# A decoder layer on one core: PSUM handed out bank by bank, gate and up products apart, waits for transfers written as pieces of their own

## The chip, the cores and the metric

The kernel runs on one core of a Trainium2 chip. The metric is the device time of one execution in microseconds; three executions of the kernel before took 1224.41 to 1229.97 us, with a median of 1229.68 us. Five engines work side by side, each through its own instructions in order: TensorE (PE, matrix products, results to PSUM), VectorE (DVE), ScalarE (ACT), GpSimd (POOL) and SyncE (SP, which here issues nearly all transfers). They wait for one another through semaphores.

## The reference

One pre-norm decoder layer on x of 4 sequences x 1024 positions x 256 channels, in float32: causal self-attention with 16 heads of 16 channels, cross-attention to a context of 77 positions with a mask, and a gated feed-forward layer of 768 hidden channels with integer weights. Cut to what is computed:

```python
Q, K, V = x @ Wq.T + bq, x @ Wk.T + bk, x @ Wv.T + bv      # per head h
scores = (gt * (Q @ W_cross) @ K.T + (1 - gt) * Q @ (M @ K).T) * scale
attn = softmax(where(causal, scores, -inf)); out = (attn @ V) @ Wo.T + bo
...
q, k, v = query @ Wq, ctx @ Wk, ctx @ Wv                   # cross-attention
attn = softmax(where(masked, -1e9, q @ k.T / sqrt(16))); out = (attn @ v) @ Wo
...
h = silu(x @ wg.T) * (x @ wu.T); out = h @ wd.T            # feed-forward
...
x = x + self_attn(layernorm(x))
x = x + cross_attn(layernorm(x), ctx, mask)
x = x + ffn(layernorm(x))
```

## The kernel before

The 4 sequences are each cut into two chunks of 512 rows, so there are eight chunks (b, n). For each chunk six things happen. `project` normalises the rows, transposes them and makes q, k and v; q and k are split into a high and a low part (`spread`), which are copied by transfers into the row layout that the score products read. `maxima` multiplies q by k and takes each row's maximum on VectorE (L879), which `shift` turns into a tile of shifts. `attend` computes the scores again the other way round, adds the shifts by another product (L955), takes the exponential on ScalarE (L968) and multiplies by v (`weigh`, L992); `quotients` divides, and `out_proj` multiplies by the output weights and adds the residual (L722). `cross_attention` does the same against the context, with score maxima at L1114 and L1120. `ffn` computes gate and up products for six blocks of 128 hidden channels (L1229), tanh on ScalarE (L1235), two multiplications on VectorE (L1236, L1237), a split into high and low parts on ScalarE and GpSimd (L1239, L1240), and then the down products (L1263), which VectorE adds to x (L1269).

The order of TensorE's instructions is not that of these functions. Each function is a generator that yields pieces. A piece states how long TensorE needs for it (`pe`), which engines work on its result and for how long (`use`), which buffers it takes, and from what time on (`at`) or under what condition (`cond`) it may start. `weave` keeps a planned time for every engine and buffer and always writes next the piece that could start first, after a small correction per stream and chunk (`LATES`). What is written is then fixed: on the chip each engine runs its instructions in that order and waits by semaphores. Work of other engines that belongs to a piece is written with it, so it also stands in the order in which pieces are chosen.

PSUM has eight banks of 512 float32 values per partition. Before, three pairs of banks (`pair`) and two single banks (`single`) are rotating buffers, and the planner keeps the same numbers of slots:

```python
pp = ctx.enter_context(tc.tile_pool(name="pp", bufs=3, space=PSUM))
ps = ctx.enter_context(tc.tile_pool(name="ps", bufs=2, space=PSUM))
...
"pair": Slots(3), "single": Slots(2), "es": Slots(6), ...
```

A gate product and its up product share one pair; so do the four row blocks of `out_proj`, of the v projection and of the down products, each of which is read by one VectorE instruction of 1024 columns (v: four ScalarE copies).

Three further places matter. In `late_weights` the selection tiles `sel` and `selB` (L524 to L536) are made after the first head group of `maxima` has been started (flag "begun"), and the mask of the first sequence (L1047 to L1049) inside `load_cross`. `load_ffn` loads, converts and transposes the feed-forward weights from the flag "selections" on. In `attend` the residual rows x are loaded and the bias `bo_b` is added to them on GpSimd (L922) at the chunk's first head group. A layer norm is statistics on VectorE (L153, L154, L156), a power on GpSimd (L158) and four normalisations on VectorE (L166), written in one go.

Of the kernel before, what the change touches and what calls it, by code (L numbers as in the profile page):

```python
# [8 lines left out]
F32 = mybir.dt.float32  # L9
# [4 lines left out]
AF = mybir.ActivationFunctionType  # L14
# [13 lines left out]
def tile_decoder_layer(  # L28
# [53 lines left out]
    pp = ctx.enter_context(tc.tile_pool(name="pp", bufs=3, space=PSUM))  # L82
    ps = ctx.enter_context(tc.tile_pool(name="ps", bufs=2, space=PSUM))

    def pair():
        return pp.tile([P, 2, CH], F32, tag="pair", name="pair")

    def single():
        return ps.tile([P, CH], F32, tag="single", name="single")
# [81 lines left out]

    def layer_norm(xt, keep=None):

        mv, rs = row_scales(xt, keep)
        return normal_rows(xt, mv, rs, wide([P, QT, D], "xn"))
# [215 lines left out]
    class Slots:  # L391
# [12 lines left out]

    slots = {
        "pair": Slots(3), "single": Slots(2), "es": Slots(6), "w4": Slots(6), "f2": Slots(6),
# [50 lines left out]
    def give(token, when):  # L457
        pool, k = token
        pool.free[k] = when
# [7 lines left out]
    def weave(*streams, until=None):  # L467
        while True:
# [23 lines left out]
            s.got = {k: [slots[k].take() for _ in range(c)] for k, c in p["take"].items()}  # L492
            s.end = t + p["pe"]
            if p["pe"]:
                if t - tensor["end"] > REST:
                    tensor["slow"] = t + COLD
                s.end += min(max(tensor["slow"] - t, 0.0) / 2, p["pe"])
                tensor.update(end=s.end, mode=p["mode"])
# [39 lines left out]
    def late_weights(st):  # L538

        yield piece(0.0, w4=1, use=[("DVE", 4.0)], cond=lambda: "begun" in flags)  # L540
        selections(wide([P, NHP, P], "sel_f"))
        st.release("w4")
        flags.add("selections")
        nc.gpsimd.memset(mneg, 0.0)
        nc.gpsimd.memset(xpad, 0.0)
        nc.gpsimd.tensor_copy(k2s, zero.to_broadcast(k2s.shape))
        nc.gpsimd.memset(v2, 1.0)
        nc.sync.dma_start(xwo, xWo.rearrange("(n p) f -> p n f", p=P))
        yield piece(0.0, w4=3, use=[("DMA", 4.0), ("POOL", 8.0)])
        toks = st.got["w4"]  # L550
        reorder(xwq, raw_weights(xWq))
        give(toks.pop(), st.done)
        raw = raw_weights(xWk)
# [3 lines left out]
        yield piece(0.0, es=2, use=[("DMA", 4.0)])  # L557
# [43 lines left out]
        yield piece(0.0, w4=2, use=[("DMA", 4.0)])  # L601
# [22 lines left out]
    def load_ffn(st, m, rest=None):  # L624
# [5 lines left out]
        for part, n0 in enumerate(range(0, n_all, step)):  # L630
            n = min(step, n_all - n0)
            yield piece(
                0.0, w4=1, use=[("DMA", 4.0), ("POOL", 1.1), ("DVE", 1.1)],
                cond=lambda: "selections" in flags,
# [5 lines left out]
            wf = wi.bitcast(F32)  # L640
            nc.gpsimd.tensor_copy(wf, wi)
# [54 lines left out]
    NORM = [("DVE", 2.6), ("POOL", 1.1), ("DVE", 1.7)]  # L696

    def out_proj(st, nat, t_nat, w, xt):
# [7 lines left out]
        for i in range(QT):  # L706
            if i % 2 == 0:
                yield piece(
                    2.0, at=st.done + LATE if i == 0 else 0.0,
                    use=[("DVE", 1.25)] if i else [], free=t_aT if i else [],  # L710
                    **({} if i else {"pair": 1}),
                )
                if i == 0:
                    t_pair = st.got["pair"]
                    t = pair().rearrange("p a (i d) -> p (a i) d", d=D)
            for c in range(NC):
                nc.tensor.matmul(
                    t[:, i, :], aT[:, c, i * P : (i + 1) * P], w[:, c, :],
                    start=(c == 0), stop=(c == NC - 1),
                )  # L720
        give(t_pair.pop(), st.done)
        nc.vector.tensor_tensor(xt, t, xt, ALU.add)  # L722
# [57 lines left out]
    def project(st, b, n):  # L780
# [4 lines left out]
        else:  # L785
            yield piece(
                0.0, use=[("DMA", 4.0)] * (b > 0) + NORM, w4=1,
# [3 lines left out]
            xn = x01 if (b, n) == (0, 1) else x_rows(b, n)  # L791
            normal_rows(xn, *row_scales(xn))
# [8 lines left out]
        for c in range(NC):  # L801
# [8 lines left out]
            if c == 0:  # L810
                for i in range(QT):
                    if i % 2 == 0:
                        yield piece(
                            2.0, use=[("ACT", 1.8)] if i else [],
                            cond=lambda: (b, n) != (0, 0) or ("normal", 0, 1) in flags,
                            **({} if i else {"pair": 1, "v": 1}),
                        )
                        if i == 0:
                            t_pair, t_v = st.got["pair"], st.got["v"][0]
                            vs = qk.tile(  # L820
                                [P, QT, H * V1 + W - V1], F32, tag="v", name="vs", bufs=NQ
                            )
                            nc.gpsimd.memset(vs, 1.0)
                            t = pair().rearrange("p a (i d) -> p (a i) d", d=D)
                    for k in range(NC):
                        nc.tensor.matmul(
                            t[:, i, :], xnT[:, k, i * P : (i + 1) * P], wvT[:, k, :],
                            start=(k == 0), stop=(k == NC - 1),
                        )
                give(t_pair.pop(), st.done)  # L830
                for i in range(QT):
                    nc.scalar.copy(
                        vs[:, i, : H * V1].rearrange("p (h w) -> p h w", w=V1)[:, :, 0:HD],
                        t[:, i, :].rearrange("p (h w) -> p h w", w=HD),
                    )
# [531 lines left out]
```

## Time and profile before

| what | value |
|---|---|
| median of three executions | 1229.68 us |
| the profiled execution | 1232.86 us |
| its span, first to last instruction | 1231.1 us |
| mean granted TensorE clock | 0.958 |
| transfers | 76.44 MB in 65438 packets |

A group row of the profile holds line, engine, operation, tiles, shapes and count, then busy time and mean duration in ns, then the idle time of the engine just before them and what ended most of it. Rows of the timeline hold start, duration and what ran; a bracket holds the idle time before it and the instruction that ended it. Ends of matmuls are modelled, so that starts tell more of their pace than durations do.

### The profile page before, as it was taken

To read this page: it belongs to the slowest core of one execution; us is meant where nothing else is said; L and a number is where in the kernel's file an instruction comes from. 1 tells how busy PE (TensorE), PEld (TensorE's weight loads), DVE (VectorE), ACT (ScalarE), POOL (GpSimd) and SP (SyncE) were. 2 spreads that over 40 slices of the span, in tenths; PEclk is the share of its full clock that TensorE was granted. 3 is DMA by queue.
4 is the path that set the end of the run, shared out by engine and by line. 5 is a ranking of instruction groups with operands and counts; after the bars stand their busy time and mean duration, and the time that the engine had idled before them with its cause. 6 is when DMAs were issued, how large, how long until landed. Compare 5 with 4: busy or idle time off the path is not lost. (4 is left out here: it accounts for less than half of the span.)

```text
span 1231.1 us, 22029 instructions
## 1 busy us (share of the span) xinstructions
PE 1110.8 (90%) x9059; PEld 684.9 (56%) x9059; DVE 729.9 (59%) x1247; ACT 562.6 (46%) x801; POOL 130.8 (11%) x138
## 2 busy tenths in 40 slices
PE   6679989999999898999898998999999889996875
PEld 4445544557555466557555456556575545565654
DVE  5566786354687856255777856347458666136342
ACT  3044544654434463753353563653535336661521
POOL 4031000002000012001100002000110000011212
PEclk9798999999999999999999998999999989998986
DMA  6992315537732016555533015444826140006000
GB/s 124 130 201 63 58 33 69 69 53 92 97 55 40 9 38 110 75 71 87 87 52 38 8 42 70 85 63 60 102 44 91 36 63 8 18 1 86 1 35 19
DMA packets 65438, 76.44 MB, mean 62 GB/s; under 512 B 22451, under 2 KB 39399, under 8 KB 65332
## 3 DMA queue, kind: packets, MB, share of 16 engines
q1 hardware_dynamic: 64227, 74.62, 39.1%
q8 instruction: 73, 1.20, 0.5%
q10 hardware_dynamic: 1104, 0.35, 0.1%
q14 instruction: 34, 0.27, 0.1%
HBM read 15.28 MB, written 9.33 MB: 20 GB/s over the span
## 5 line engine op out<-in xcount | busy, mean ns | idle before, releaser
L968 ACT ACTIVATE es<-pair 128x1024 f32<-128x1024 f32 (+3 forms) x384 | 300.8, 812 | 252.6 <-PE pair L962 178.4
L879 DVE TENSOR_REDUCE mt<-pair 128x2 f32<-128x1024 f32 (+3 forms) x384 | 351.4, 952 | 92.3 <-PE pair L874 60.8
L866 PE MATMUL pair<-k,q 64*128 64x512 f32 (+3 forms) x768 | 163.2, 428 | 29.8 <-DVE mt L879 12.6
L949 PE MATMUL pair<-q,k 64*128 64x512 f32 (+3 forms) x768 | 161.4, 417 | 22.4 <-DVE mt L879 16.5
L992 PE MATMUL single<-es,vs 128*32 128x512 f32 (+3 forms) x1536 | 166.2, 506 | 0.1
L866 PEld LDWEIGHTS pair<-k,q 64*128 64x128 f32 x768 | 76.0, 188 | 121.4 <-DVE mt L879 41.7
L955 PE MATMUL pair<-ms,sel 64*128 64x512 f32 (+3 forms) x768 | 134.6, 347 | 0.0
L949 PEld LDWEIGHTS pair<-q,k 64*128 64x128 f32 x768 | 73.2, 187 | 102.6 <-issue 34.8
L1240 POOL TENSOR_TENSOR hT<-h,hT 128x512 fp32r<-128x512 f32 x48 | 61.4, 1280 | 306.8 <-ACT hT L1239 297.2
L1162 ACT ACTIVATE es<-pair 77x1024 f32<-77x1024 f32 x64 | 63.4, 1020 | 45.8 <-PE pair L1160 45.5
L955 PEld LDWEIGHTS pair<-ms,sel 64*128 64x128 f32 x768 | 74.2, 190 | 3.1
L1120 DVE TENSOR_REDUCE mx<-pair 128x8 f32<-128x616 f32 x64 | 48.7, 794 | 43.7 <-PE pair L1114 43.7
L1263 PE MATMUL pair<-wdT,hT 128*128 128x256 f32 x384 | 63.3, 320 | 11.6 <-POOL hT L1240 4.8
L158 POOL TENSOR_TENSOR rs<-ve,mhalf 128x4 f32<-128x4 f32 x24 | 24.3, 1012 | 439.5 <-DVE ve L156 439.4
L1235 ACT ACTIVATE h<-pair 128x512 f32<-128x512 f32 x48 | 28.7, 598 | 89.0 <-PE pair L1229 84.8
L874 PE MATMUL pair<-cm_qk,id 64*128 64x64 bf16 (+1 forms) x1024 | 69.0, 211 | 0.0
L962 PE MATMUL pair<-cm_kq,id 64*128 64x64 bf16 (+1 forms) x1024 | 67.3, 211 | 0.0
L1236 DVE SCALAR_TENSOR_TENSOR h<-h,pair 128x512 f32<-128x512 f32 x48 | 33.0, 687 | 57.5 <-ACT h L1235 57.2
L1263 PEld LDWEIGHTS pair<-wdT,hT 128*128 128x128 f32 x384 | 55.8, 216 | 18.4 <-POOL hT L1240 6.3
L1114 PE MATMUL pair<-k2s,q 128*128 128x156 f32 x256 | 46.7, 308 | 12.1 <-DMA q<-hi 5.3
L992 PEld LDWEIGHTS single<-es,vs 128*32 128x32 f32 x1536 | 32.4, 109 | 40.7 <-issue 29.6
L674 ACT COPY aS<-single 128x512 f32<-128x512 f32 x64 | 37.5, 589 | 31.6 <-PE single L992 19.0
(180 smaller groups left out, 1575.0 us busy)
## 6 DMA issues: line engine op xcount, KB each, us to landing
q<-hi SPq DMA_DIRECT2D x128, 128.0 KB, 5.1
q<-lo SPq DMA_DIRECT2D x128, 128.0 KB, 6.3
k<-hi SPq DMA_DIRECT2D x64, 128.0 KB, 4.3
k<-lo SPq DMA_DIRECT2D x64, 128.0 KB, 6.0
xr<-in_x_dram SPq DMA_DIRECT2D x8, 512.0 KB, 6.0
x<-in_x_dram SPq DMA_DIRECT2D x8, 512.0 KB, 7.4
x_dram<-x SPq DMA_DIRECT2D x8, 512.0 KB, 2.6
out_dram<-x SPq DMA_DIRECT2D x8, 512.0 KB, 3.7
```

The lines of the kernel that those rows point to most:

```text
L866: nc.tensor.matmul(t[:, j, :w], q[r, a, i * P : (i + 1) * P], k[r, a, :w], start=True, stop=True,)
L874: nc.tensor.matmul(t[:, j, w - P + 64 * half : w], id2[r, half], cm_qk[r, half, 64 * half :], start=False, stop=True, skip_group_check=True,)
L879: nc.vector.tensor_reduce(mt[:, i, :, p, kc], t[:, :, :w], AX.X, ALU.max)
L949: nc.tensor.matmul(t[:, j, lo:], k[r, a, ki * P : (ki + 1) * P], q[r, a, lo:], start=True, stop=False,)
L955: nc.tensor.matmul(t[:, j, lo:], sel[r, hp, :], ms[r, lo:], start=False, stop=True)
L962: nc.tensor.matmul(t[:, j, lo : lo + 64 * (half + 1)], id2[r, half], cm_kq[r, half, : 64 * (half + 1)], start=False, stop=True, skip_group ...
L968: nc.scalar.activation(es[:, :, lo:], t[:, :, lo:], AF.Exp)
L992: nc.tensor.matmul(acc[0][W * jj : W * (jj + 1), lo:], vs[:, ki, V1 * h : V1 * h + W], both[jj // 2][:, jj % 2, lo:], start=(kb == 0), sto ...
L1120: nc.vector.tensor_reduce(mt[:, i, h4 : h4 + 4, :].rearrange("q (k p) j -> q k (p j)", k=2), tv[:, :, :, :S2], AX.X, ALU.max,)
L1162: nc.scalar.activation(es[:S2], t[:S2], AF.Exp)
L1240: nc.gpsimd.tensor_tensor(hs[:, 1, :], h, hs[:, 0, :].bitcast(F32), ALU.subtract)
L1263: nc.tensor.matmul(t[:, i, :], h[1][:, v, i * P : (i + 1) * P], w[:, h[0], :], start=(m == 0), stop=(m == len(terms) - 1),)
```

## The change

PSUM becomes one tile of eight banks. The planner's `Banks` keeps one list of eight times when banks come free; a single takes the highest bank that is free by the plan, a pair two neighbours, even positions first. The gate product and the up product take a single each; `out_proj`, the v projection and the down products are made in two halves of one bank each, with one VectorE or ScalarE instruction per half. When the planner sees TensorE stand still for over 1.3 us and a bank is free, `stirred` writes filler products into the bank about to be used; the next product overwrites them. Statistics and normalisation, loads and the work on what they bring, become separate pieces. The selections and the first mask are made ahead of the first maxima, the feed-forward weights are loaded after the first attention, and x and its bias come at the last head group. The planned transfer time goes from 4.0 to 6.5 us in these pieces, and `LATES` has other values.

```diff
-    pp = ctx.enter_context(tc.tile_pool(name="pp", bufs=3, space=PSUM))
-    ps = ctx.enter_context(tc.tile_pool(name="ps", bufs=2, space=PSUM))
+    pp = ctx.enter_context(tc.tile_pool(name="pp", bufs=1, space=PSUM))
+    banks = pp.tile([P, 8, CH], F32, name="banks")
...
+    def stirred(t, part):
+        for _ in range(int(stand["us"] / 0.235)):
+            nc.tensor.matmul(part, selB, sel[:, 0:4, :], start=True, stop=True)
+        stand["us"] = 0.0
+        return t
+
+    def bank(kind, of):
+        if given[kind]:
+            return given[kind].pop(0)
...
     def pair():
-        return pp.tile([P, 2, CH], F32, tag="pair", name="pair")
+        b = bank("pair", 4)
+        return stirred(banks[:, b : b + 2, :], banks[:, b, :])
...
+    class Banks:
...
+        def take(self):
+            now = max(tensor["end"], self.when(1))
+            ready = [b for b in self.all() if self.at(b) <= now]
+            b = max(ready) if self.width == 1 else min(ready, key=lambda b: (b % 2, b))
+            self.give(b, 1.0e9)
+            return self, b
...
-        "pair": Slots(3), "single": Slots(2), "es": Slots(6), "w4": Slots(6), "f2": Slots(6),
+        "pair": Banks(free_banks, 2), "single": Banks(free_banks, 1), "es": Slots(6), "w4": Slots(6), "f2": Slots(6),
...
             if p["pe"]:
-                if t - tensor["end"] > REST:
+                idle = t - tensor["end"]
+                early = max([slots[k].when(1) for k in ("pair", "single") if k in p["take"]] or [t])
+                if idle > REST and early < tensor["end"] + 0.5 and "selections" in flags:
+                    stand["us"] = idle - 0.7
+                elif idle > REST:
                     tensor["slow"] = t + COLD
...
-        yield piece(0.0, w4=1, use=[("DVE", 4.0)], cond=lambda: "begun" in flags)
+        yield piece(0.0, w4=1, use=[("DVE", 5.5)], cond=lambda: ("normal", 0, 1) in flags)
         selections(wide([P, NHP, P], "sel_f"))
...
+        cross_mask(0)
+        flags.add("selections")
+        yield piece(0.0, cond=lambda: "begun" in flags)
...
             yield piece(
-                0.0, w4=1, use=[("DMA", 4.0), ("POOL", 1.1), ("DVE", 1.1)],
-                cond=lambda: "selections" in flags,
+                0.0, w4=1, use=[("DMA", 6.5)], cond=lambda: ("attended", 0, 0) in flags
             )
...
+            yield piece(
+                0.0, use=[("POOL", 1.1), ("DVE", 1.25)], at=st.done if st else 0.0
+            )
             nc.gpsimd.tensor_copy(wf, wi)
...
-        give(t_pair.pop(), st.done)
-        nc.vector.tensor_tensor(xt, t, xt, ALU.add)
+        at = st.done + LATE
+        for half in range(2):
+            yield piece(2.0, at=at, use=[("DVE", 0.7)], free=t_aT * half, single=1)
+            t = single().rearrange("p (i d) -> p i d", d=D)
...
+            part = xt[:, 2 * half : 2 * half + 2, :]
+            nc.vector.tensor_tensor(part, t, part, ALU.add)
+            st.release("single")
...
-            xn = x01 if (b, n) == (0, 1) else x_rows(b, n)
-            normal_rows(xn, *row_scales(xn))
+            xn = x_rows(b, n) if b else x01
+            yield piece(0.0, use=STATS, at=st.done)
+            scales = row_scales(xn)
+            yield piece(0.0, use=[("DVE", 1.5)], at=st.done)
+            normal_rows(xn, *scales)
...
-                if g == 0:
-                    yield piece(0.0, x=1, use=[("DMA", 4.0)])
...
+                if g == NG - 1 and kb == 0:
+                    yield piece(0.0, x=1, use=[("DMA", 6.5)])
+                    xt = xpool.tile([P, QT, D], F32, tag="x", name="x", bufs=3)
...
         yield from lag.pop()()
+        yield piece(0.0, use=[("POOL", 2.4)], at=x_at)
+        nc.gpsimd.tensor_tensor(xt, xt, bo_b.unsqueeze(1).to_broadcast([P, QT, D]), ALU.add)
...
             for k in range(2):
                 yield piece(
...
+                    0.95, at=at, single=1, free=t_x if k and hc == NH - 1 else [],
+                    use=[("DVE", 0.7), ("ACT", 0.5), ("POOL", 1.3)] if k else
+                    [("ACT", 0.6), ("DVE", 0.75)],
+                    **({"es": 1} if k else {"f2": 1}),
+                )
+                t = single()
...
+                if k == 0:
+                    h = wk2.tile([P, CH], F32, tag="f2", name="h", bufs=6)
+                    t_h = got("f2")
+                    nc.scalar.activation(h, t, AF.Tanh, scale=0.5 / 127.0)
+                    nc.vector.scalar_tensor_tensor(h, h, 1.0, t, ALU.add, ALU.mult)
+                    release("single")
+            nc.vector.tensor_tensor(h, h, t, ALU.mult)
...
-                nc.vector.scalar_tensor_tensor(
-                    xt, t, 0.5 / 127.0**3, xt, ALU.mult, ALU.add
-                )
+                    part = xt[:, 2 * half : 2 * half + 2, :]
+                    nc.vector.scalar_tensor_tensor(
+                        part, t, 0.5 / 127.0**3, part, ALU.mult, ALU.add
+                    )
+                    release("single")
```

## The prediction

> **What bounds the kernel now.** I read the page first: engine shares and granted clock.
>
> ```profile
> PE 1110.8 (90%) x9059; PEld 684.9 (56%) x9059; DVE 729.9 (59%) x1247; ACT 562.6 (46%) x801; POOL 130.8 (11%) x138
> PEclk9798999999999999999999998999999989998986
> ```
>
> PE is the bound at 90%, with 1231.1 - 1110.8 = 120.3 us idle. The clock row shows that PE's work is dear at both ends. The windows view splits this into three stages (us busy and count by engine, then granted clock, DMA share, GB/s):
>
> ```profile
> 0.00:100.00 100.00, 72.08 (x531) 45.24 (x532) 59.51 (x125) 28.77 (x52) 25.51 (x46) 0.85 0.83 140
> 100.00:1100.00 1000.00, 943.22 (x8040) 567.53 (x8041) 609.47 (x1013) 498.10 (x696) 80.35 (x71) 0.98 0.38 58
> 1100.00:1231.10 131.10, 95.46 (x490) 72.13 (x489) 60.94 (x110) 35.73 (x53) 24.91 (x21) 0.85 0.18 33
> ```
>
> PE stands still for 28 us in the first 100, 57 in the next 1000 and 36 in the last 131: over half of the idle time lies in a fifth of the span. The chain of waits gives only the last 4 us, so the last stage has to be read from the timeline (start, us, what; the brackets hold the idle time before it):
>
> ```profile
> 1187.03 1.94 PE L182 MATMUL pair<-ident,xn 128*128 128x128 f32 x8 [4.93 <-DVE xn L166]
> ...
> 1191.33 0.79 PE L1229 MATMUL pair<-xl,wgT 128*128 128x512 f32 x1 [0.47 <-DVE xl L1209]
> 1191.92 0.63 PE L1229 MATMUL pair<-xh,wgT 128*128 128x512 f32 x1
> 1192.35 0.63 PE L1229 MATMUL pair<-xl,wgT 128*128 128x512 f32 x1
> ...
> 1196.33 0.39 PE L1229 MATMUL pair<-xh,wuT 128*128 128x512 f32 x1
> 1196.56 0.39 PE L1229 MATMUL pair<-xl,wuT 128*128 128x512 f32 x1
> ```
>
> See the starts: 0.43 us apart after the stop, 0.23 later. A stop costs itself and then half-speed matmuls. In the body two rows tell how the other engines hold PE:
>
> ```profile
> L879 DVE TENSOR_REDUCE mt<-pair 128x2 f32<-128x1024 f32 (+3 forms) x384 | 351.4, 952 | 92.3 <-PE pair L874 60.8
> L166 DVE TENSOR_SCALAR xn<-x,mv,rs x64: 395/407/2407, 152.2 to 1187.4; 128x256 f32<-128x256 f32 x64
> ```
>
> The reduce is DVE's largest load, and it releases PSUM pairs. The second row (min/median/max in ns) shows a 0.4 us operation that once took 2.4 us: by the timeline it started at 984.55, beside GpSimd's 2.34 us bias add (L922, from 984.47).
>
> **The last layer, 1182.1 to 1225.0 (42.9 us).** It is a serial chain, so I walk it with the built order of the changed kernel: eight products of the last projection, then 26 fillers, 8 transposes, 9 fillers, 24 gate/up matmuls, 16 down, 16 gate/up, 5 fillers, 16 down, 8 gate/up, 13 fillers, 16 down. A filler has the operand size of a gate/up matmul, 0.233 us warm. After the projection: 26 fillers 6.1 us. They cover half an add (0.69), statistics and power (1183.39 to 1186.43, 3.0) and four normalisations (1.4), so they are 0.9 too long. Transposes 1.2: at 7.3. Nine fillers 2.1 stand over the cast (1.01) and the subtraction (1.23): at 9.5. 24 x 0.233 = 5.6: 15.1. Down products 2.0 plus 0.4 for GpSimd's last part: 17.5. Then 3.7 + 1.2 + 2.0: 24.4. The last gate/up 1.9: 26.3. Gate now has its own bank, so tanh (0.60) and the first multiply (0.69) run under the up matmuls; what remains is 0.69 + 0.61 + 1.28 and some 0.2 of hand-over, 2.8, while 13 fillers take 3.0: 29.3. Down 2.0, half an add 0.8: **32.1 us, a gain of 11**.
>
> Here a rule bears. The Trainium skill, "TensorE: Matmul & The Clock Gate", section "HAM oscillation — how this bites in real kernels", states that idle gaps over about 3.4 us cost the clock. By it, only the 4.93 us stop is worth filling: ten gate matmuls and the transposes, 10 x 0.2 + 0.9 = 3 us, and the short filler groups would be pure cost. The rows say otherwise: starts are 0.43 apart again from 1203.75 and 1212.99, after stops of 0.69 + 1.02 and 1.02 + 0.96 us. That is 13 x 0.2 = 2.6 us, and about 1.5 for the final down products. I take the rows (7 us from the clock, 4 from the shorter chain); by the rule the stage gains 7.
>
> **1100 to 1178.** One stop counts: 5.33 us before the cross scores (L1114) for the transfer of q, then 1.26 for its second half, with half clock from 1123.8 to 1130.6. The new order puts another 16 down products (2.0 us) into it, then 5 + 4 fillers, and 11 before the second half. The transfer stays; 2.0 of work moves under it and 6.8 x 0.45 = 3 us of half speed goes; fillers may overrun by 1: **-4** (bounds -7, +1).
>
> **The start.** Selections and the first mask (L524 to L536, L1047 to L1049: some 4 us of DVE) move from 49 to 53 us, where PE stops 1.70 and 1.62 us for L879, to about 30 us, where DVE waits for work until 39.8. Gain 3.3. Price: 12 fillers need sel, ready at about 32, and last 2.8 (warm) to 5.1; the second query and next key projections (1.9 each) follow and end near 40. First scores start at 38.07 in the trace, held by q<-lo; they now start 1 to 3 later, but a key projection that took 2.88 at 43.34 is done by then. On SP nothing shifts: the query rows queue there until 39.94 anyhow. **-4** (bounds -8, +3).
>
> **The body.**
> - Statistics and normalisation become two pieces, so reduces may stand between; DVE sat 22.5 us in 20 waits for GpSimd's power before L166. The bias add also moves to the end of an attention. On GpSimd it waited 155.9 us for its x load, with powers and memsets queued behind it; now it is written when the load has landed. On SP that load moves to the last head group, behind more q/k rows: 7.4 us to landing, needed only after the last products, so it stays covered; if not, the first sum of out_proj and the cross-attention behind it are late by the rest. The stop that both explain is 3.80 us at 984.8, and 6.9 us at half clock after it: 3.8 + 2.5 = -6.3.
> - Feed-forward weights wait for the first attention to end. On DVE six reduces (2.4 + 1.9 + 1.4 us), on GpSimd their casts and on SP 12 loads leave the stage with stops of 3.19 and 1.09: -3. They land where PE is 98% busy and DVE under half.
> - Halving projections and sums costs DVE. Row: 1.22 us for 1024 columns against 2 x 0.684 for 512 from PSUM: 0.146 more, 40 times, 5.9 us. "Perfetto Trace Analysis", section "Optimizing Scalar/DVE Operations", speaks against it: about 125 ns per DVE instruction on PSUM, group operations where the engine is saturated: 5.0. Row taken. About 200 more DVE semaphore waits, 21 ns each by the trace, 4 us. With DVE 61% busy here I charge a fifth: +2.
> - Bank by bank: PE waits for DVE and ACT at L866 and L949 are 39 us in total. In the built orders, returns of PSUM with under 1 us of matmul work since the producing matmul go from 124 to 118 for DVE and from 73 to 119 for ACT. So the freedom is spent on tighter use. No row of before shows the result: bounds -8 (a fifth of 39) and +23 (46 more at 0.5 us, half an exponential of 1.03). I take 0, since fewer of one kind stand against more of the other.
> Sum **-7** (bounds -18, +17).
>
> **The sum** is -11 - 4 - 4 - 7 = -26 us. It is made against the profiled execution, 1232.86 us (span 1231.1), which lies 3.2 above the median of 1229.68. The same gain from the median gives **1204 us**.
>
> **Rivals.**
> 1. *Ends only.* The body gives back what it gains: DVE pays all of the 10 us, two fifths of it on the path, and no stop goes. Start and end gain 19, the body costs 4: 1215 us. For it: the tighter ACT returns. Against: the 3.80 us stop has a cause that the change removes.
> 2. *Slower.* The bank taken is the lowest that the plan thinks free, not the one free longest; PE's order is fixed, so where the exponential is later than planned PE stops. Price: 46 short returns at 0.6 to 0.8, some 32 us, and five more half-clock windows (3.4 x 0.45 = 1.5), 8 us: +40, less 19 at the ends and 5 in the body, 1246 us. It decides once the short returns cost over 30 us. For it: 73 to 119. Against: the older kernel had 197 such returns of both kinds and 39 us of waits.
> 3. *Nothing moves.* Fillers overrun their stops at the true durations and hold back the work behind them, so that the 19 at the ends shrink to 6, and the body costs 4: about 1228 us. The 0.9 us above is such a case.
>
> **Chances.** Forecast 0.53 (own range 1192 to 1215), ends only 0.17, nothing 0.10, slower 0.20. A measurement tells 0.5%, 6 us, from no change: faster 0.70, same 0.10, slower 0.20. The range reaches to 1186 (a body at its better bound) and to 1238 (part of rival 2).
>
> **What would show it.** Right: in the last stage no matmul starts 0.43 apart, and 32 us from the last projection to the end; PE's clock near full from 1100 on; no stops near 50 us; L166 never over 1 us. Wrong: PE idle before attention scores and maxima with ACT es as releaser well above 10 us; fillers that end later than the operation they cover; DVE busy over 745.

## The result, and the profile after

The changed kernel took **1211.11 us** (median of four executions, 1210.83 to 1215.41) against 1229.83 us for the kernel before on the same chip (1224.41 to 1231.24). The ratio is 0.985, with a 95% interval from 0.983 to 0.988: 18.7 us faster, where 26 were forecast. The profiled execution took 1210.99 us, with a span of 1209.2.

From the profile's page of the changed kernel, the busy row and the clock row:

```profile
PE 1115.3 (92%) x9147; PEld 685.7 (57%) x9147; DVE 730.2 (60%) x1287; ACT 559.6 (46%) x785; POOL 131.0 (11%) x138
PEclk9899999999999999989999999999899999999999
```

PE's count has grown by 88, which are the fillers. Its idle time is 1209.2 - 1115.3 = 93.9 us; it was 120.3. DVE runs 40 more instructions and is busy for the same time as before (729.9). The last 11 digits of the clock row are 9, where the last four were 8986.

The windows view of the changed kernel by stage (as before: us busy and count by engine, then granted clock, DMA share, GB/s):

```profile
0.00:100.00 100.00, 79.74 (x638) 49.27 (x638) 67.42 (x134) 32.38 (x53) 22.49 (x43) 0.93 0.88 139
100.00:1100.00 1000.00, 941.41 (x7987) 565.44 (x7986) 606.22 (x1052) 493.85 (x683) 86.39 (x78) 0.98 0.37 58
1100.00:1209.20 109.20, 94.10 (x526) 70.99 (x524) 56.59 (x103) 33.39 (x50) 22.14 (x18) 0.98 0.22 40
```

The last stage is 22 us shorter with nearly the same PE time, at a clock of 0.98 instead of 0.85. In the middle PE is busy for as long as before (941 and 943 us), and runs 53 matmuls fewer. So I cut the span at three events that both kernels have:

| event | before | after | gain in the stretch that ends there |
|---|---|---|---|
| last attention score starts | 1091.8 | 1084.3 | 7.5 |
| last projection ends | 1182.1 | 1168.6 | 6.0 |
| last sum ends | 1225.0 | 1202.3 | 9.2 |

The last 118 us hold two thirds of the gain (15.2 of 22.7; 0.8 is lost after the last sum). The 7.5 us of the first stretch are not spread over it. By 100 us the changed kernel has issued 626 products besides its 12 fillers there, the one before 531. To follow this lead I weigh every product by the mean time from one start to the next that its kind has in three traces (before, changed, changed without fillers), leave fillers out, and ask when the kernel before had done as much. This is an estimate; other ways of weighing move it by up to 2 us. At 100 us the changed kernel is 9 us ahead, at 300 us 7 behind, at 900 us still 7 behind, at 1000 us 6 ahead, at 1060 us 8 ahead. The body as a whole has gained nothing: it gives the lead of the start back and wins it again late.

The timeline of the last layer in the changed kernel (start, us, what; the brackets hold the idle time before it):

```profile
1168.25 6.26 PE L93 MATMUL banks<-sel,selB 128*128 128x512 f32 x26
1174.35 1.03 PE L197 MATMUL banks<-ident,xn 128*128 128x128 f32 x8
1175.14 2.35 PE L93 MATMUL banks<-sel,selB 128*128 128x512 f32 x9
...
1183.17 0.51 PE L1296 MATMUL banks<-xh,wuT 128*128 128x512 f32 x1 [0.75 <-DVE h L1306]
1183.52 0.39 PE L1296 MATMUL banks<-xl,wuT 128*128 128x512 f32 x1
...
1185.24 1.82 PE L1331 MATMUL banks<-wdT,hT 128*128 128x256 f32 x13 [0.52 <-POOL hT L1309]
```

No stop is longer than 0.75 us, and gate and up products follow one another mostly at 0.23 us; no run of them is 0.43 apart. But the transposes no longer have a bracket at all: the fillers themselves (L93) hold them back, which matters below.

Two more rows answer to those shown of before. The group row of the reduce, on the page:

```profile
L938 DVE TENSOR_REDUCE mt<-banks 128x2 f32<-128x1024 f32 (+3 forms) x384 | 349.8, 952 | 99.8 <-PE banks L933 65.8
```

And the range of the normalisations, from the view of their line (min/median/max in ns):

```profile
L186 DVE TENSOR_SCALAR xn<-x,mv,rs x64: 381/407/1364, 150.3 to 1172.6; 128x256 f32<-128x256 f32 x64
```

The reduce is as it was. The normalisation that once took 2407 ns now takes 1364 at most.

### The profile page after: what moved, and what is told of

Its sections match the earlier page's. It is cut to its first block, busy times and chain, and to the rows that moved or that the text cites. A ratio compares the mean times of both kernels' runs of the same rounds, so it can differ in the third digit from the quotient of the medians.

```text
span 1209.2 us, 22461 instructions
## 1 busy us (share of the span) xinstructions
PE 1115.3 (92%) x9147; PEld 685.7 (57%) x9147; DVE 730.2 (60%) x1287; ACT 559.6 (46%) x785; POOL 131.0 (11%) x138
## 4 chain that ended last, share of the span: by engine, by line
PE 67%; DVE 11%; DMA 11%; ACT 6%; issue 2%; POOL 2%; SPq 1%; ACTq 0%; DVEq 0%; POOLq 0%
PE banks L1041 10%; PE banks L998 7%; PE banks L925 6%; PE banks L1296 6%; PE banks L819 5%; PE banks L1004 4%; DMA q<-lo 4%; PE banks L769 4%; DVE mt L938 4%; PE banks L1226 4%; PE banks L1331 3%; DMA k<-lo 3%; ACT es L1017 3%; PE banks L1239 3%; PE banks L197 2%
## 5 line engine op out<-in xcount | busy, mean ns | idle before, releaser
L1017 ACT ACTIVATE es<-banks 128x1024 f32<-128x1024 f32 (+3 forms) x384 | 298.6, 811 | 243.6 <-PE banks L1011 162.5
L938 DVE TENSOR_REDUCE mt<-banks 128x2 f32<-128x1024 f32 (+3 forms) x384 | 349.8, 952 | 99.8 <-PE banks L933 65.8
L925 PE MATMUL banks<-k,q 64*128 64x512 f32 (+3 forms) x768 | 163.6, 427 | 27.5 <-DVE mt L938 15.8
L998 PE MATMUL banks<-q,k 64*128 64x512 f32 (+3 forms) x768 | 161.9, 414 | 18.0 <-DVE mt L938 5.9
L1041 PE MATMUL banks<-es,vs 128*32 128x512 f32 (+3 forms) x1536 | 167.1, 508 | 1.9 <-ACT aS L730 0.8
L925 PEld LDWEIGHTS banks<-k,q 64*128 64x128 f32 x768 | 75.2, 187 | 115.6 <-DVE mt L938 42.6
L1004 PE MATMUL banks<-ms,sel 64*128 64x512 f32 (+3 forms) x768 | 136.6, 348 | 2.2 <-DVE ms L804 2.2
L998 PEld LDWEIGHTS banks<-q,k 64*128 64x128 f32 x768 | 74.4, 188 | 98.4 <-ACT es L1017 36.5
L1228 ACT ACTIVATE es<-banks 77x1024 f32<-77x1024 f32 x64 | 63.1, 1018 | 34.5 <-PE banks L1226 34.1
L1004 PEld LDWEIGHTS banks<-ms,sel 64*128 64x128 f32 x768 | 75.5, 190 | 5.9 <-DVE ms L804 2.5
L933 PE MATMUL banks<-cm_qk,id 64*128 64x128 bf16 (+1 forms) x1024 | 67.9, 211 | 0.0
```

Of the source, the lines that this page charges most:

```text
L925: nc.tensor.matmul(t[:, j, :w], q[r, a, i * P : (i + 1) * P], k[r, a, :w], start=True, stop=True,)
L933: nc.tensor.matmul(t[:, j, w - P + 64 * half : w], id2[r, half], cm_qk[r, half, 64 * half :], start=False, stop=True, skip_group_check=True,)
L938: nc.vector.tensor_reduce(mt[:, i, :, p, kc], t[:, :, :w], AX.X, ALU.max)
L998: nc.tensor.matmul(t[:, j, lo:], k[r, a, ki * P : (ki + 1) * P], q[r, a, lo:], start=True, stop=False,)
L1004: nc.tensor.matmul(t[:, j, lo:], sel[r, hp, :], ms[r, lo:], start=False, stop=True)
L1017: nc.scalar.activation(es[:, :, lo:], t[:, :, lo:], AF.Exp)
```

## The experiments

Each table row gives the median, the ratio to the kernel before on the same chip with its 95% interval, and from the profiled execution PE's idle time (span less busy), the mean clock and the length of the last layer, from the end of the last projection to the end of the last sum. (The expectations name 33.9 or 34.1 us for the changed kernel's last layer, which take in small instructions behind the last sum; it is 33.7.) Kernels of different groups ran on different chips (the kernel before took 1229.4 to 1231.4 there), so ratios compare best.

| kernel | us | ratio | PE idle | clock | last layer |
|---|---|---|---|---|---|
| before | 1229.83 | 1 | 120.3 | 0.958 | 42.9 |
| changed | 1211.11 | 0.985 [0.983, 0.988] | 93.9 | 0.979 | 33.7 |
| changed, no fillers | 1216.06 | 0.988 [0.986, 0.990] | 106.6 | 0.968 | 34.5 |
| before + fillers | 1253.64 | 1.019 [1.016, 1.021] | 117.3 | 0.970 | 38.5 |
| before + late pieces | 1308.79 | 1.062 [1.059, 1.065] | 157.3 | 0.929 | 42.1 |
| before + banks | 1255.22 | 1.019 [1.016, 1.021] | 137.4 | 0.958 | 34.9 |
| before, table 0 | 1314.17 | 1.069 [1.063, 1.075] | 172.2 | 0.934 | 42.2 |
| before + banks, table 0 | 1282.10 | 1.043 [1.038, 1.049] | 152.3 | 0.949 | 34.1 |
| before + late pieces, table 0 | 1332.38 | 1.083 [1.077, 1.088] | 172.9 | 0.921 | 41.0 |
| changed, table 0, no fillers | 1261.93 | 1.024 [1.020, 1.028] | 140.7 | 0.954 | 34.7 |
| changed, table 0 | 1264.50 | 1.027 [1.022, 1.033] | 119.1 | 0.965 | 33.6 |
| changed, short fillers | 1210.81 | 0.983 [0.980, 0.986] | 96.4 | 0.971 | 31.8 |
| changed, tanh issued late | 1211.13 | 0.984 [0.981, 0.987] | 92.9 | 0.976 | 33.7 |
| changed, gate second | 1216.26 | 0.989 [0.985, 0.993] | 94.6 | 0.976 | 39.5 |

"Banks" stands for PSUM bank by bank with the split products, "late pieces" for the work behind transfers in pieces of its own and all that moves with it, "table" for `LATES`.

### Without the fillers

The plan is the same, only the fillers are not written:

```diff
-        for _ in range(int(stand["us"] / 0.235)):
+        for _ in range(0):
```

> The changed kernel without its 88 filler products (order, banks and LATES as they are). Theory (clock by the rows): the end stage runs its matmuls 0.43 us apart again after each stop; the last layer, from the last projection to the last sum, goes from 34.1 to 40 us or more, and the whole from 1211 to about 1219. Rival (the skill's gap of about 3.4 us): only the long stop after the last projection matters, 1214. Rival (the fillers only stand in the way): the same or faster, 1209 to 1211.

It took 1216.06 us, and its profiled span is 4.3 us longer than the changed kernel's (1213.5). The intervals of the two ratios overlap a little, so 4 to 5 us is the size, with some doubt. By the three events: the last attention score starts at 1084.2, as with fillers, so the 12 fillers at the start brought nothing that lasts; the last projection ends at 1172.2, 3.6 later; the last layer takes 34.5, 0.8 more, and not the 40 or more that was expected. Its timeline, the same stretch:

```profile
1175.68 1.95 PE L197 MATMUL banks<-ident,xn 128*128 128x128 f32 x8 [3.53 <-DVE xn L186]
1178.74 0.79 PE L1296 MATMUL banks<-xh,wgT 128*128 128x512 f32 x1 [1.10 <-ACT xh L1277]
1180.00 0.79 PE L1296 MATMUL banks<-xl,wgT 128*128 128x512 f32 x1 [0.47 <-DVE xl L1279]
...
1188.44 1.81 PE L1331 MATMUL banks<-wdT,hT 128*128 128x256 f32 x13 [0.65 <-POOL hT L1309]
```

Here the stops are seen bare. The one after the last projection is 3.53 us; the 26 fillers, with the matmul's end before them, keep the transposes waiting from 1168.60 to 1174.35, 5.75 us. So they overrun by 2.2 us. Without them the transposes take 1.95 instead of 1.03 us and the clock of the layer is 0.85 instead of 1.00. That costs little more than the overrun, as the layer is only 0.8 us longer. Even so the layer is 8.4 us shorter than before the change: most of its gain is not the fillers'.

### One part at a time, with the older table

Each kernel is the one before with one part of the change, cut to its core here. Fillers alone, on the older pairs and singles:

```diff
+        return stirred(t, t[:, 0, :])
...
+                if idle > REST and early < tensor["end"] + 0.5 and "selections" in flags:
+                    stand["us"] = idle - 0.7
```

Late pieces alone, with selections, mask, x and weights at their new places:

```diff
+            yield piece(0.0, use=STATS, at=st.done)
+            scales = row_scales(xn)
+            yield piece(0.0, use=[("DVE", 1.5)], at=st.done)
```

Banks alone, with all the products that the change splits:

```diff
-        "pair": Slots(3), "single": Slots(2),
+        "pair": Banks(free_banks, 2), "single": Banks(free_banks, 1),
```

> The kernel before with the fillers alone: the planner's rule for stops and the filler products, PSUM, splits and pieces as before. Theory: the clock's share of the ends, some 7 us, comes without any other part: 1222. Rival (fillers pay only together with the shorter chains): 1228 to 1230. Rival (the filler holds back the work behind it, as the older plan puts its stops elsewhere): over 1232.

> The kernel before with the late-written pieces alone: statistics and normalisation apart, selections and first mask early, weights after the first attention, x and bias at the last head group, 6.5 us for transfers; three pairs and two singles, no fillers, the older LATES. Theory (prediction): start and the 3.80 us stop go, -8 to -13, so 1217 to 1222. Rival (the order is only shuffled, as the equal attention marks up to 830 us say): within 4 us of 1229.

> The kernel before with bank by bank alone: one tile of eight banks, gate and up products apart, projections and down products by halves; no fillers, no late pieces, the older LATES. Theory (prediction): the shorter gate/up chain gives some 4 us at the end and the body about +2: 1226 to 1230. Rival (tight returns of banks cost): 1240 or more, with more idle of PE before L998 and L925 on the exponential. Rival (eight banks free the body): 1215 or less.

All three were slower than before, by 23, 79 and 25 us, though together, with the newer table, they are 19 us faster. The last layer tells that the parts did their work: 38.5 us with fillers alone, 34.9 with banks alone. The loss lies ahead of it: the last attention score starts at 1113.5, 1167.4 and 1124.2, instead of 1091.8. With fillers alone the body has a few fillers and otherwise the same pieces in another plan: where it fills a stop, it no longer counts on a slow clock behind it, and orders the pieces otherwise. With banks alone the rival's sign, waits for the exponential, came too: those of the score products rise from 9.7 to 20.4 us, while their waits for the reduce fall from 29.1 to 20.8. That leaves most of the 25 us open. I suspected the table: its values correct the planned times of one set of pieces, and need not suit another.

### The same with the table at 0

```diff
-    LATES = (
...
+    LATES = ([0.0] * 8, [0.0] * 8, [0.0] * 8, [0.0] * 4, [0.0] * 4, [0.0] * 8)
```

> The kernel before with every entry of its table of delays set to 0; nothing else. Theory O (the order that the table makes is worth tens of microseconds, and each part tried alone lost it because the older table fits only the older pieces): the time rises by 20 to 60 us, to 1250 to 1290, the same rise as the three single parts showed (23 to 79). Theory S (the parts themselves are slow when alone, the table is worth little): the time stays within 8 us of 1230.

> The changed kernel with every entry of the table set to 0; nothing else. Theory O: 20 to 50 us slower than the changed kernel, 1231 to 1261, and below the kernel before with zeros by about what the structure is worth, 10 to 25 us. Theory S: within 8 us of 1211.

> The kernel before with only bank-by-bank PSUM and the split products, and the table at 0. Compared with the kernel before with zeros. Theory O with a gain from the banks: 5 to 15 us faster than that, since a matmul piece waits for one bank and not for a pair. Theory O without one: within 8 us, as the sums by piece are the same. Rival (shorter returns of banks and twice the VectorE instructions cost): 5 to 25 us slower.

> The kernel before with only the late-written pieces (a transfer's consumer in a piece of its own, scales and rows apart, the weights of the feed-forward later), and the table at 0. Compared with the kernel before with zeros. If the late pieces are where the gain of the body lies: 5 to 20 us faster. If they are only useful with the split products: within 8 us, or slower. If the 79 us of the older table's run come from the pieces themselves, it is again 40 us or more slower.

> The changed kernel with the table at 0 and no fillers: banks and late-written pieces together. With zeros the kernel before took 1314, banks alone 1282, late pieces alone 1332, all with fillers 1264.5. If the parts add up: 1300 (1314 - 32 + 18), and the fillers are worth 36 us there. If the late pieces gain once a bank is enough for a piece: 1268 to 1280, and the fillers are worth 4 to 15, near the 5 us that they were worth in the changed kernel.

Without its table the kernel before takes 1314 us: the table is worth 85 us to it. To the banks alone the same table is worth 27 us (1282.1 to 1255.2) and to the late pieces alone 24 (1332.4 to 1308.8). So the older table suits the older pieces best, as theory O has it, with a size beyond the 20 to 60 us expected. The changed kernel loses 53 us without its own, and is then 50 us faster than the kernel before without its table, where 10 to 25 were expected.

With the table at 0 no part has a table made for other pieces. Banks alone: 32 us faster than 1314.2, where 5 to 15 were expected. Late pieces alone: 18 slower. Both: 1261.9, lower than either expectation, which is 20 faster than banks alone, so in these orders the late pieces gain once the banks are there; the sum of the two single effects would have been 1300. Fillers on top: no gain that can be told from none (1264.5, with overlapping intervals), although idle time falls from 140.7 to 119.1 us: the fillers count as busy. Each of these kernels is one order out of many, though. The tables alone, which change nothing but the order, move the time by 24 to 85 us, and no run shows how far another order of the same pieces would land. So 32, 18 and 20 us are differences between orders, and not yet what a part is worth.

The views of waits show the exchange (line that waits, what it waits for: us in total, times, longest). Before with table 0:

```profile
PE pair L866 <- DVE mt L879: 25.0, 33, 7.5
PE pair L949 <- DVE mt L879: 13.1, 23, 1.3
PE single L747 <- DVE xpad L1126: 7.3, 2, 6.0
...
PE pair L866 <- DMA q<-lo: 4.7, 2, 3.9
```

With late pieces alone:

```profile
PE pair L870 <- DVE mt L883: 26.4, 44, 2.5
PE single L747 <- DVE xpad L1137: 16.0, 7, 3.9
PE pair L870 <- DMA q<-lo: 15.0, 10, 4.3
...
PE pair L943 <- DVE mt L883: 8.6, 14, 1.1
```

With banks alone:

```profile
PE banks L921 <- DVE mt L934: 12.4, 29, 1.4
...
PE banks L1004 <- ACT es L1023: 7.5, 21, 0.8
...
PE banks L1004 <- DVE mt L934: 1.9, 2, 1.3
```

With banks and late pieces, no fillers:

```profile
PE banks L925 <- DMA q<-lo: 11.2, 8, 3.5
PE banks L925 <- DVE mt L938: 8.6, 25, 0.7
...
PE banks L998 <- ACT es L1017: 6.3, 16, 0.8
PE banks L998 <- DVE mt L938: 2.5, 2, 1.9
```

L866, L870, L921 and L925 are the same score product ahead of the maxima, L949, L943, L1004 and L998 the one in `attend`. Neither reads what the reduce `mt` writes; they wait for the PSUM that the reduce has read. With pairs that costs 38 us, or 35 with late pieces; with banks alone it costs 14.3, with banks and late pieces 11.1. So it is the banks that take these waits away. All waits for the exponential `es` rise meanwhile, from 12.8 us with pairs to 20.4 with banks and late pieces. Late pieces on pairs add waits for transfers and for the padded tile of the cross-attention (`xpad`), and take little off the returns.

### Shorter fillers

```diff
-        for _ in range(int(stand["us"] / 0.235)):
+        for _ in range(int(0.55 * stand["us"] / 0.235)):
```

> The changed kernel with every group of fillers cut to 0.55 of its length (26 become 14, 12 become 7, 13 become 7); the order of all other TensorE work is the same. Theory L (the fillers are longer than the stops: the group of 26 took 6.26 us, and without any filler that stop was 3.53; the groups of 9 and 13 overran by about 1 us each): 2 to 5 us faster than the changed kernel, 1206 to 1209, with the last layer at 30 to 32 us instead of 33.9. Theory C (the full length is needed to hold the clock): half speed returns in the last layer, and the time is 1211 to 1216.

The order of all other TensorE work is that of the changed kernel. The last layer fell to 31.8 us with the clock at 1.00 in it, as theory L has it: 14 fillers are enough. The whole did not follow: 1210.81 us, and its interval overlaps with that of the changed kernel by half. In the profiled execution the 1.9 us were lost elsewhere. The timelines of both at the same stop; first the changed kernel, then the one with shorter fillers:

```profile
318.86 0.45 PE L998 MATMUL banks<-q,k 64*128 64x384 f32 x2 [2.12 <-DVE x L1336]
...
319.51 1.06 PE L1041 MATMUL banks<-es,vs 128*32 128x512 f32 x8
```

```profile
318.29 0.69 PE L998 MATMUL banks<-q,k 64*128 64x384 f32 x2 [2.12 <-DVE x L1336]
...
319.41 1.93 PE L1041 MATMUL banks<-es,vs 128*32 128x512 f32 x8
```

There is no filler near; the stop is 2.12 us in both. One execution went on at full speed, the other at half speed for 10.2 us, and by three eighths of the attention scores it was 4 us late. So a gain of 2 us at the end is real in the timeline and below what the total can show here.

### The gate's tanh, tried twice

In the last layer alone, the gate's tanh and its product are issued after the up product, and the bank is planned as taken until then:

```diff
-                    nc.scalar.activation(h, t, AF.Tanh, scale=0.5 / 127.0)
-                    nc.vector.scalar_tensor_tensor(h, h, 1.0, t, ALU.add, ALU.mult)
-                    release("single")
+                    gate, t_gate = t, list(got("single"))
+                if k == last:
+                    nc.scalar.activation(h, gate, AF.Tanh, scale=0.5 / 127.0)
+                    nc.vector.scalar_tensor_tensor(h, h, 1.0, gate, ALU.add, ALU.mult)
...
```

> The changed kernel, where in the last layer alone the gate's tanh and its product are issued after the up product's matmuls, as they were before the change; the two products keep a bank each. The order of the TensorE work is the same everywhere. Theory E (the early tanh on the gate's own bank is what shortened the last layer, 42.9 to about 34.5 without any filler): the last layer grows by 3 to 6 us, to 37 to 40, and the whole to 1214 to 1217. Theory H (the halves of the projection and of the sums did it, or the banks' earlier return): the last layer stays within 1.5 us of 33.9 and the whole within 2 us of 1211.

It changed nothing: 33.7 us, 1211.13. The timeline of ScalarE shows why, and that this run doesn't decide between the theories:

```profile
1179.14 0.60 ACT L1307 ACTIVATE h<-banks 128x512 f32<-128x512 f32 x1 [2.31 <-PE banks L1298]
```

The gate's last matmul started at 1178.71 and the up product's first at 1178.94. ScalarE had nothing else to do, so the tanh ran as early as before, wherever it was written. In the kernel before, with gate and up in one pair, the first tanh started at 1194.78, after the up product, as did all 48 of that kernel; in the changed one 3 of 48 did. To make it late, the second run puts the up product first:

```diff
-                terms = [(w, v, c) for w in parts[k] for c in range(NC) for v in (hi, lo)]
+                terms = [
+                    (w, v, c) for w in parts[k ^ last] for c in range(NC) for v in (hi, lo)
+                ]
```

> The changed kernel, where in the last layer alone the up product comes first and the gate's second, so that the tanh can't start before both are done. (With the gate's tanh only issued later, it still ran as soon as the gate's four matmuls were done, 1179.14 us after 1178.94, so that run told of the bank's return alone.) Before the change the tanh started after the up product, too (first tanh at 1194.78, last up matmul of the pair started at 1194.05). Theory E (the tanh's early start is what shortened the last layer): the chain behind the second product is longer by tanh and product, 0.60 + 0.69 us, before each of three groups of down products, so the last layer grows by 2.5 to 4.5 us from 33.9 and the whole to 1213 to 1216. Theory H (the clock and the halves of the projection and the sums did it): the last layer stays within 1 us of 33.9 and the whole within 2 us of 1211.

The last layer grew from 33.7 to 39.5 us, more than theory E asked for, and the whole to 1216.26. Two of its stops in the timeline:

```profile
1184.77 0.85 PE L1340 MATMUL banks<-wdT,hT 128*128 128x256 f32 x5 [0.96 <-POOL hT L1318]
1187.01 1.69 PE L1340 MATMUL banks<-wdT,hT 128*128 128x256 f32 x8 [1.38 <-DVE h L1313]
1188.50 0.63 PE L1300 MATMUL banks<-xh,wuT 128*128 128x512 f32 x1
1188.92 0.63 PE L1300 MATMUL banks<-xl,wuT 128*128 128x512 f32 x1
```

The stops of 0.96 and 1.38 us are followed by starts 0.43 apart; a half-speed window of 3.4 us is recorded from 1187.5. In the changed kernel the layer has no such window. But the 1.38 us is a down product that waits for a bank, since the third product of h came after a sum on DVE in this kernel: its input was ready at 1184.59, it started at 1186.27. The layer can be cut by group of down products. The first group takes 3.0 us longer than in the changed kernel, with that wait in it, and the 16 products behind it 1.0 longer, at half speed. The second and third group, without such a wait and at full speed, take 0.9 longer each. So an early tanh is worth about 0.9 us in each of these two groups. If it is in the first as well, that makes some 2.8 of the 5.8, an estimate, and the rest is the wait and the clock that it cost.

No kernel tried was measurably faster than the changed one.

## Why the prediction was right, and where its steps were off

The forecast was faster, 1204 us, within 1186 to 1238; it came to 1211. The 7 us have two sources. The sum of 26 us was too large by 4: the span fell by 21.9, and that 4 is itself the rest of larger errors in the start and the body, which offset. And I put a gain worked out in one profiled execution on the median: the execution of before was 3.2 us above its median, that of after at its median, so the medians differ by only 18.7.

**The last layer: -11 forecast, -9.2 measured.** The walk gave 32.1 us, the trace 33.7. The term that was mis-sized is the first run of 24 gate and up products, set at 24 x 0.233 = 5.6 us. It took 6.9 (1177.32 to 1184.21): the third up product waits 0.75 us for VectorE's multiply of the block before (the row of 1183.17 above), a wait that the walk did not have. The three groups of down products add 0.3 us each, and the beginning came 0.8 us earlier than walked (8.7 after the projection, not 9.5).

The cover of the 26 fillers, "0.9 us too long", was wrong too, though it does not enter the walk's sum, which counts the fillers whole. I put the statistics (3.0) whole behind the projection. The halves do more than I counted: DVE's timeline in the run without fillers has

```profile
1170.47 0.69 DVE L774 TENSOR_TENSOR x<-banks,x 128x512 f32<-128x512 f32 x1 [1.22 <-PE banks L769]
1171.20 0.75 DVE L173 BATCH_NORM_STATS2 st<-x 128x6 f32<-128x256 f32 x2
1171.86 0.30 DVE L174 BATCH_NORM_AGGREGATE mv<-st 128x2 f32<-128x6 f32 x2
1172.20 0.69 DVE L774 TENSOR_TENSOR x<-banks,x 128x512 f32<-128x512 f32 x1
```

with the projection's end at 1172.16: the first half's add and statistics run beside the second half's matmuls. The bare stop is 3.53 us, not 5.1, and the fillers overrun by 2.2.

The split "7 us from the clock, 4 from the shorter chain" was wrong in another way. Fillers alone take the layer from 42.9 to 38.5 us, banks and halves alone to 34.9, both to 33.7. Each was a gain; they don't add up, and of the two the layout is the larger. A likely reason is that a shorter chain leaves shorter stops, which cost less clock: the clock of the layer is 0.74 before, 0.85 in the changed kernel without fillers.

The rule that I weighed, of the Trainium skill's page "TensorE: Matmul & The Clock Gate", section "HAM oscillation — how this bites in real kernels" (idle gaps over about 3.4 us cost the clock), was rightly set aside as a bound: without fillers the stops of 1.08, 0.38 and 1.03 us ahead of the final down products are followed by half speed from 1203.0 to 1206.5. But what it gave for the fillers there, 3 us, is nearer to the 0.8 measured than my 7.

**1100 to 1178: -4 forecast, -6.0 measured** (from the last attention score to the last projection, 90.3 to 84.3). Without fillers it is 88.0, so fillers bring 3.7 and moved work 2.3. This is near the 3 and 2.0 of the working, and the overrun by 1 did not come: fillers and 1.84 us of idle time (at 1126.5) stand where the run without them stops for 4.38.

**The start and the body: -4 and -7 forecast, -7.5 together measured.** Parted at 100 us by the weighed work, the start gained about 9 us and the body lost about 1. So the start was worth twice its forecast, the body's gain did not come, and that their sum is near is luck. In the start the stops at 49 to 53 us are gone and the clock of the first 100 us is 0.93 instead of 0.85, but a stop of 2.36 us has come at 29.23 where the fillers wait for `selB`, half speed is still recorded from 48.4 to 55.3, and the run without fillers is as far by 1084. Of the body's terms:
- The stop of 3.80 us at 984.8 is gone. In the timeline of before it stands as

```profile
988.59 0.79 PE L949 MATMUL pair<-q,k 64*128 64x512 f32 x2 [3.80 <-DVE mt L879]
```

The work that lies between 980 and 1010 us there is done 9 us faster by the weighed count, more than the 6.3 of the working. All else in the body lost about 10. The longest normalisation of the form `xn` fell to 1364 ns, not below 1 us as the prediction had it for L166, and on the same line the other form, `xr`, has one of 2595 (1492 before). That one started at 24.82, beside three GpSimd instructions in a row (24.74 to 27.27). And stops of 3.34 (149.9), 3.40 (218.1) and 3.71 us (601.3) have come, which no term of mine held. They stand in the new order, with fillers and without. I costed what each edit does to the older order, and had no term for an order made anew; which of its waits cost the 10 us stays open.
- Halving: 5.9 us of DVE was right, and nearer than the 5.0 from the page that the prediction cites. The sums and additions went from 48.9 to 54.9 us. The normalisations paid it back, from 51.1 to 45.5 us for the same 96, of which 5 instead of 12 took over 1 us; DVE's busy time rose by 0.3 in all, and stays under the 745 that I had named as a sign.
- Reuse of banks at 0 (bounds -8 to +23): in the changed kernel the score products wait

```profile
PE banks L925 <- DVE mt L938: 15.8, 26, 3.7
...
PE banks L925 <- ACT es L1017: 6.9, 16, 0.8
PE banks L998 <- DVE mt L938: 5.9, 3, 3.3
PE banks L998 <- ACT es L1017: 5.1, 12, 0.9
```

With two further rows of 0.7 and 0.2 this is 34.6 us, after 38.8: fewer for the reduce (29.1 to 21.7), more for the exponential (9.7 to 12.9). The waits for ScalarE rose by 3 us, not by 32. That ends rival 2, whose text also has the bank wrong: a pair takes the lowest that is free, a single the highest. With the table at 0 the waits for the reduce fell by 27 us (38.1 to 11.1); here they fell by 7, as the older table had brought them to 29.1 in its own way, and with the newer one they are 21.7.

**The rivals.** Rival 3 fell: the ends gained 15, not 6. Rival 1, 1215 us, put the whole gain at the start and the end, 19 us, with a body that costs 4. By the weighed count these gained about 24 and the body cost 1, so in where the gain lies rival 1 is nearer than the forecast; wrong in it is "no stop goes". The forecast was right in sign and for the ends, a little high in the last layer, and wrong for the body.

## What to carry to other kernels

When a change alters what a planner orders, trying its parts one by one under corrections made for the older pieces misleads: here all three parts looked slow, and the whole was 19 us faster with its own. Compare with the corrections at 0 as well (here 50 us faster), and remember that each such run is one order, so that differences of tens of us need more than one of them. Costing the edits in the older order is not enough either; the ends, where the work is a chain, came out near the working, the body between them did not. Fillers and a shorter dependency chain both remove clock loss, so ask what each is worth with the other in place. A filler group should be no longer than the stop that the trace shows without it, and two products that share a tile may both have to be done before either is read.

## What the runs showed of the hardware that I had not expected

The same stop of 2.12 us, at the same instruction, was followed by 10.2 us at half speed in the kernel with shorter fillers (eight products in 1.93 us) and by full speed in the changed kernel (1.06 us), as also in the kernels without fillers, with the late tanh and with the gate second. There is one profiled execution of each. So the length of a short stop alone did not fix the clock's answer here, and a sum of clock losses stop by stop carries an uncertainty of several us. Stops of 0.96 and 1.38 us within 3 us were followed by a half-speed window, while in the changed kernel, with no stop over 0.75 us, the clock stayed at 1.00 over the whole last layer.

Every normalisation of over 1 us, 12 in the trace of before and 5 in that of after, ran beside GpSimd; all 17 ended 0.15 us after the end of a GpSimd instruction. So 0.41 us became 1.1 to 1.5 beside ones of 1.0 to 1.3, 2.41 beside one of 2.34, 2.59 beside three in a row. Not every GpSimd instruction does this: two normalisations beside a power of 128x4 values (at 530.6 and 530.9 us in the changed kernel) took 0.41. On the path, that is a cost of the order alone.
